# A residual convolution block with merged VectorE passes, an accumulating transfer for the input's sum, and five column-filtered positions

## The chip, the cores and the metric

The kernel runs on one core of a Trainium2 chip. The metric is the device time of one execution in microseconds (us). Before the change three runs took 1788.07, 1795.76 and 1796.89 us, with a median of 1795.76 us.

## The reference

The program is a network of four residual layers on an input of 4 images x 256 channels x 56 x 56, all in 32-bit floats. Each layer is `x = x + layer(groupnorm(x))`:

- Layers 0 and 2 are involutions: a per-pixel 7 x 7 kernel is computed from the pixel and applied to its neighbourhood.
- Layer 1, which the change is about, is a pair of 3 x 3 convolutions with batch norms:

```python
h = relu(bn(conv3x3(x, w1), g1, b1, rm1, rv1))
h = bn(conv3x3(h, w2), g2, b2, rm2, rv2)
return relu(x + h)          # x here is the group-normed input
```

  so the layer's result is `x + relu(gn(x) + bn(conv(relu(bn(conv(gn(x)))))))`.
- Layer 3 scales the input by two gates that come from means and a Fourier transform.

## The kernel before, in words

The three stages run one after the other: the involution of layer 0 (up to about 511 us), the convolutions of layer 1 (`conv_layer`, about 511 to 1241 us) and the involution of layer 2 with layer 3 folded in. Only `conv_layer` is touched by the change.

**Tiling.** 128 channels lie on the partitions, so an image has two blocks of input channels (`ci`) and two of output channels (`co`). An image is worked on in three chunks of rows, so there are 12 steps of each convolution. The first convolution takes 20, 18 and 18 rows (`C1_ROWS`), the second 16, 20 and 20 (`C2_ROWS`). The order is conv1(0), then conv1(i) and conv2(i-1) in turn, and conv2(11) at the end.

**Row filter.** Along a row, four outputs at a time are computed by a Winograd filter F(4,3): the row is split into four phases (columns 0, 1, 2, 3 modulo 4), and six linear combinations of them, the positions k = 0 to 5, are formed by VectorE (`transform`, lines 1322 to 1350; `input1` and `input2` call it for the two convolutions). For each position TensorE sums over 3 rows and 2 channel blocks: 6 matmuls for each `co`, 12 for a position (L1440 in conv1, L1522 in conv2). The six sums are then combined into the four output phases by VectorE. The positions are worked off in the order `KS = (1, 2, 3, 4, 0, 5)`. In the profile a 32-bit matmul appears as two.

**Column filter.** For three positions (`K2 = (1, 2, 3)`) conv1 is in addition filtered along columns, two output rows at a time (F(2,3)): VectorE makes four combinations of neighbouring rows (`columns`, L1374, in two halves), and TensorE needs 4 products x 4 matmuls = 16, each over half as many rows (L1411). The weights for it are made once by `column_weights` (lines 1257 to 1264). The first step, conv1(0), is not filtered, because the column weights are made during it. To evacuate a filtered position, ScalarE copies the first product (L1423) and VectorE combines it with the other three (L1426, L1427, L1429, L1430).

**What sets the order.** The program's order is written out by hand. Each step has a list `after` of 12 slots, and `after[n]` is run between the matmul groups: the transform of the step to come, the phases of the next chunk (`phases`, ScalarE, L1319, which reads the loaded rows in steps of four), the group norm's small steps (`norm_steps`, called through the list `slow` in slots 5 and 11), statistics of the finished rows (`stats`, L1565), loads and stores. `in_order` then pins the program order on every engine, so each engine works off its queue in the order of the code; an instruction that waits holds up all behind it.

**PSUM.** There are 8 banks, one to a tile (`one_bank`). A filtered position takes four. A norm step takes one from its matmul until VectorE reads it, one step's slot later.

**The end of conv2.** For each `co` ScalarE computes the residual `res = gn(x)` (L1507, `res` has one buffer), VectorE adds the four output phases to it in steps of four floats (`residual`, L1515, four passes), and one VectorE pass (L1558) computes `x + max(res, 0)`, which POOL's queue stores to HBM (L1559). `x` was loaded by `load_residual` (L1301) on SP's queue. The statistics of the result are taken in the same step for `co` = 0 and in the next conv2 for `co` = 1.

Of the kernel before, what the change touches and what calls it, by code (L numbers as in the profile page):

```python
# [16 lines left out]
P = 128  # L17
# [54 lines left out]
def net_kernel(  # L72
# [1109 lines left out]
    def conv_layer(xin, xout, st, ahead):  # L1182
        with ExitStack() as es:
            wpool = es.enter_context(tc.tile_pool(name="cw", bufs=1))
            work = es.enter_context(tc.tile_pool(name="cwork", bufs=2))
            mm_ps = es.enter_context(tc.tile_pool(name="cmm_ps", bufs=8, space=PSUM))

            def one_bank():
                return mm_ps.tile([P, 512], F32, name="mm")
# [5 lines left out]
            KS, K2 = (1, 2, 3, 4, 0, 5), (1, 2, 3)  # L1195
            u1_sb = wpool.tile([P, NB, 3, WPOS, C], F32, name="u1_sb")
            ux_sb = wpool.tile([P, NB, len(K2), C], F32, name="ux_sb")
            u2_sb = wpool.tile([P, NB, 3, WPOS, C], F32, name="u2_sb")


# [9 lines left out]
            last_y = wpool.tile([P, NY], F32, name="last_y")  # L1210

            def y_tile(k):
                if k < 5:
                    return room["h"][:, k * NY : (k + 1) * NY]
                return room["xr"][:, 2 * NX : 2 * NX + NY] if k == 5 else last_y
# [40 lines left out]

            def column_weights(ci, k0, k1):

                w0, w1, w2 = (u1_sb[:, ci, y, k0:k1, :] for y in range(3))
                x = ux_sb[:, ci, k0 - 1 : k1 - 1, :]  # L1260
# [5 lines left out]

            ph1 = wpool.tile([P, 4, CV_ROWS + 2, NB, WT + 1], F32, name="ph1")
            nc.gpsimd.memset(ph1[:, 0, :, :, 0:1], 0.0)
            nc.gpsimd.memset(ph1[:, 1, :, :, WT : WT + 1], 0.0)
            ph2 = wpool.tile([P, 4, H + 2, NB, WT + 1], F32, name="ph2")  # L1270
            nc.gpsimd.memset(ph2[:, 0, :, :, 0:1], 0.0)
            nc.gpsimd.memset(ph2[:, 1, :, :, WT : WT + 1], 0.0)
# [30 lines left out]
            def phases(i):  # L1303
# [8 lines left out]
                for ci in range(NB):  # L1312
                    at = ci * (CV_ROWS + 2) * W
                    xr = room["rows"][:, at : at + (hi - lo) * W].rearrange("p (r t j) -> p j r t", t=WT, j=4)
                    for j in range(4):
                        q, t0 = (j + 1) % 4, (j + 1) // 4
                        dst = ph1[:, q, r0 : r0 + hi - lo, ci, t0 : t0 + WT]
# [4 lines left out]
            def transform(v, ph, n):  # L1322

                by = [ph[:, j].rearrange("p r c t -> p (r c) t") for j in range(4)]
                d = [t[:, :, :WT] for t in by] + [t[:, :, 1:] for t in by[:2]]
                vs = [v[:, k, : n * NB] for k in range(WPOS)]
                stt(vs[4], d[2], -4.0, d[4], ALU.mult, ALU.add)
                yield
                stt(vs[3], d[1], -4.0, d[3], ALU.mult, ALU.add)
                yield  # L1330
                tt(vs[1], vs[4], vs[3], ALU.add)
                yield
                tt(vs[2], vs[4], vs[3], ALU.subtract)
                yield
                tt(vs[3], d[4], d[2], ALU.subtract)
                yield
                tt(vs[4], d[3], d[1], ALU.subtract)
                yield
                tt(vs[0], d[0], d[2], ALU.subtract)
                yield  # L1340
                stt(vs[0], vs[3], 0.25, vs[0], ALU.mult, ALU.add)
                yield
                tt(vs[5], d[5], d[3], ALU.subtract)
                yield
                stt(vs[5], vs[4], -4.0, vs[5], ALU.mult, ALU.add)
                yield
                stt(vs[3], vs[4], 2.0, vs[3], ALU.mult, ALU.add)
                yield
                stt(vs[4], vs[4], -4.0, vs[3], ALU.mult, ALU.add)
                yield  # L1350
# [5 lines left out]
            def input1(i):  # L1356
                y0, y1, _, _ = rows1(i)
                n = y1 - y0 + 2
                yield from transform(new_v((1, i)), ph1[:, :, :n], n)

            def input2(i):
                y0, y1 = C2_ROWS[i % 3]
                yield from transform(new_v((2, i)), ph2[:, :, y0 : y1 + 2], y1 - y0 + 2)

            def columns(i, k, half):
# [3 lines left out]
                v = v_of[1, i][:, k].rearrange("p (r e c) t -> p e r (c t)", e=2, c=NB)  # L1369
                d = [v[:, 0, :m], v[:, 1, :m], v[:, 0, 1 : m + 1], v[:, 1, 1 : m + 1]]  # L1370
                t = v2_of[i, k, half] = new_v2().rearrange("p (e r n) -> p e r n", e=2, n=NB * WT)
                pairs = ((1, 2, ALU.add), (2, 1, ALU.subtract)), ((0, 2, ALU.subtract), (1, 3, ALU.subtract))
                for e, (p, q, op) in enumerate(pairs[half]):
# [384 lines left out]
```

## Time and profile before

| | |
|---|---|
| median of three runs | 1795.76 us (1788.07 to 1796.89) |
| profiled execution | 1790.97 us |
| its span, first to last instruction | 1788.9 us |
| mean granted TensorE clock | 0.983 |
| TensorE matmul busy | 1719.6 us (96%) |
| VectorE busy | 1385.5 us (77%) |
| ScalarE busy | 814.5 us (46%) |
| GpSimd (POOL) busy | 377.3 us (21%) |
| stretch of the convolutions | about 511 to 1241 us |

PE is TensorE's matmul row, PEld its weight loads, DVE VectorE, ACT ScalarE, POOL GpSimd and SP the queue that issues most transfers. In a line of a group, the numbers after the count are the busy time in us and the mean length of one in ns, then the idle time before it and who ended it. In a timeline the first number is the start and the second the length, in us. Instructions on one engine overlap a little: the distance from start to start is what one costs in a full queue.

### The profile page before, as it was taken

Reading aid. Unit: us, or ns where it says so; the run is one execution under the profiler, and the core shown is the slowest. Engines: PE = TensorE matmul, PEld = TensorE weight load, DVE = VectorE, ACT = ScalarE, POOL = GpSimd, SP = SyncE. Lnnn points to the kernel's source line nnn. Section 1 sums busy time; section 2 is a strip of 40 time slices with the busy share of each in tenths; the row PEclk is TensorE's granted clock in tenths of the full one; section 3 lists DMA queues with packets and bytes.
Section 4 is the critical chain, followed back from the end, with each engine's and each line's share of the span. In section 5 each row is a group of like instructions: output and inputs, shape, how many; then the busy total and the mean of one; then the engine's idle time right before and its main releaser. Section 6 shows DMA issues by size and latency. Waiting matters only on the chain.

```text
span 1788.9 us, 55629 instructions
## 1 busy us (share of the span) xinstructions
PE 1719.6 (96%) x24040; PEld 1510.4 (84%) x24040; DVE 1385.5 (77%) x2745; ACT 814.5 (46%) x1882; POOL 377.3 (21%) x571
## 2 busy tenths in 40 slices
PE   6999999999999999999999999999999999899898
PEld 4988988989978988898889888986888887788786
DVE  2677787767778988988898889885787787677675
ACT  2655556555533223231323132112767567567564
POOL 2223321333210000000000000001000464553572
PEclk9999999999989999999999999999999999999996
DMA  2345444634653121211111111122345566665653
GB/s 86 127 159 166 137 151 136 197 107 131 208 158 104 39 67 57 71 43 54 64 64 46 50 64 37 45 111 72 126 161 166 166 215 206 194 202 186 181 157 114
DMA packets 67907, 215.74 MB, mean 121 GB/s; under 512 B 12790, under 2 KB 20479, under 8 KB 63951
## 3 DMA queue, kind: packets, MB, share of 16 engines
q1 hardware_dynamic: 54750, 159.83, 28.4%
q0 software_dynamic: 11072, 50.32, 8.2%
q8 instruction: 189, 3.10, 0.7%
q10 hardware_dynamic: 1840, 2.05, 0.4%
q14 instruction: 56, 0.45, 0.1%
HBM read 76.30 MB, written 49.15 MB: 70 GB/s over the span
## 4 chain that ended last, share of the span: by engine, by line
PE 68%; DVE 18%; DMA 4%; issue 4%; ACT 3%; POOL 1%; SPq 1%; ACTq 0%; DVEq 0%; POOLq 0%
PE mm L1522 17%; PE ps L592 14%; PE ps L634 13%; PE mm L1440 10%; DVE kt L610 5%; PE mm L1411 5%; DMA xw<-xw 4%; PE ps L406 3%; DVE un L654 3%; PE ps L468 2%; DVE res L1515 1%; DVE xs L1374 1%; DVE st L1104 1%; ACT hp L487 1%; PE ps L717 1%
## 5 line engine op out<-in xcount | busy, mean ns | idle before, releaser
L634 PE MATMUL ps<-kt,xw 126*32 126x48 f32 (+1 forms) x12544 | 379.9, 235 | 25.9 <-issue 13.4
L634 PEld LDWEIGHTS ps<-kt,xw 126*32 126x32 f32 (+1 forms) x12544 | 341.2, 121 | 71.5 <-issue 49.9
L592 PE MATMUL ps<-hp,z_sb 64*126 64x133 f32 x6144 | 384.1, 279 | 8.8 <-DVE kt L610 5.1
L592 PEld LDWEIGHTS ps<-hp,z_sb 64*126 64x126 f32 x6144 | 364.5, 186 | 24.7 <-DVE kt L610 6.9
L1522 PE MATMUL mm<-v,u_sb 128*128 128x280 f32 (+1 forms) x1728 | 383.5, 383 | 1.9 <-DVE u_sb L1253 1.5
L610 DVE TENSOR_TENSOR kt<-ps,zb_sb 126x798 f32<-126x798 f32 x352 | 333.0, 980 | 60.4 <-PE ps L592 60.1
L1522 PEld LDWEIGHTS mm<-v,u_sb 128*128 128x128 f32 x1728 | 326.1, 189 | 56.3 <-DVE u_sb L1253 1.9
L603 ACT ACTIVATE kt<-ps,zb_sb 126x133 f32<-126x133 f32 x960 | 280.8, 442 | 107.6 <-PE ps L592 107.6
L1440 PE MATMUL mm<-v,u_sb 128*128 128x252 f32 (+1 forms) x936 | 209.5, 384 | 0.0
L1440 PEld LDWEIGHTS mm<-v,u_sb 128*128 128x128 f32 x936 | 176.4, 189 | 30.5 <-issue 0.8
L654 DVE SCALAR_TENSOR_TENSOR un<-ps,s,un 128x240 f32<-128x240 f32 x224 | 102.5, 458 | 85.2 <-ACT un L649 78.8
L654 DVE SCALAR_TENSOR_TENSOR un<-ps,par_sb,un 128x240 f32<-128x240 f32 x224 | 97.7, 456 | 83.7 <-ACT un L647 79.8
L1559 POOL DMA_DIRECT2D x<-xs x24 | 13.2, 548 | 681.3 <-DVE xs L1558 426.5
L1507 ACT ACTIVATE res<-xs,shift,norm_sb 128x1120 f32<-128x1120 f32 (+1 forms) x24 | 30.2, 1258 | 236.9 <-DVE xs L1558 107.3
L418 ACT COPY xw<-ps 126x896 f32<-126x896 f32 x112 | 101.4, 906 | 40.7 <-PE ps L406 21.3
L659 POOL TENSOR_TENSOR xs<-un,xs 128x240 f32<-128x240 f32 x112 | 72.2, 666 | 218.6 <-DVE un L654 218.6
L406 PE MATMUL ps<-ident_sb,strip_sb 128*126 128x128 f32 x784 | 111.0, 282 | 5.3 <-issue 1.7
L647 ACT ACTIVATE un<-ps,par_sb 128x240 f32<-128x240 f32 x112 | 50.3, 449 | 120.5 <-PE ps L634 106.9
L649 ACT ACTIVATE un<-ps,bn_t,s 128x240 f32<-128x240 f32 x112 | 60.0, 538 | 92.8 <-PE ps L634 82.0
L1411 PE MATMUL mm<-xs,u_sb 128*128 128x126 f32 (+1 forms) x792 | 98.7, 277 | 2.0 <-DVE xs L1427 1.0
L406 PEld LDWEIGHTS ps<-ident_sb,strip_sb 128*126 128x126 f32 x784 | 84.3, 141 | 16.5 <-POOL strip_sb L391 4.2
L1411 PEld LDWEIGHTS mm<-xs,u_sb 128*128 128x128 f32 x792 | 94.4, 191 | 3.3 <-DVE xs L1427 1.6
(255 smaller groups left out, 1882.2 us busy)
## 6 DMA issues: line engine op xcount, KB each, us to landing
xw<-xw SPq DMA_DIRECT2D x224, 252.0 KB
xw<-xw SPq DMA_DIRECT2D x224, 126.0 KB
xs<-x SPq DMA_DIRECT2D x24, 560.0 KB
x<-xs POOLq DMA_DIRECT2D x8, 1568.0 KB, 7.8
xs<-x SPq DMA_DIRECT2D x8, 1568.0 KB
xs<-in_x_dram SPq DMA_DIRECT2D x6, 1568.0 KB
x<-xs SPq DMA_DIRECT2D x6, 1568.0 KB
gx<-x POOLq DMA_DIRECT2D x42, 224.0 KB, 5.2
```

What stands on the lines that cost most here:

```text
L406: nc.tensor.transpose(ps[:Q, k * P : (k + 1) * P], flat[:, k * Q : (k + 1) * Q], ident_sb)
L418: nc.scalar.copy(xw[:, :NSB, :], ps[:Q, : NSB * P].rearrange("q (n c) -> q n c", n=NSB))
L592: nc.tensor.matmul(ps[:Q, i, k * NT : (k + 1) * NT], z_sb[i * R : (i + 1) * R, cb * GB // 2 + gp, z0 : z0 + Q], hp[i * R : (i + 1) * R, py ...
L603: nc.scalar.activation(kt[:, g0 + i, pb, :, k], ps[:Q, i, k * NT : (k + 1) * NT], AF.Identity, bias=zb_sb[:, cb * GB + g0 + i, p0 + k : p0 ...
L610: nc.vector.tensor_tensor(kt[:, g0 : g0 + 2, pb], ps[:Q, :, : PB * NT].rearrange("q i (k t) -> q i t k", k=PB), zb_sb[:, cb * GB + g0 : cb ...
L634: nc.tensor.matmul(v[m * j : m * j + m, i, :, k * TP : (k + 1) * TP], xw[:, window(ty), m * j : m * j + m], kt[:, ng * j : ng * j + ng, :, ...
L649: nc.scalar.activation(part, o[0], AF.Identity, bias=bn["t4"][:, cb : cb + 1], scale=bn["s4"][ng][:, 0, cb : cb + 1])
L654: nc.vector.scalar_tensor_tensor(part, o[e], s, part, ALU.mult, ALU.add)
L659: nc.gpsimd.tensor_tensor(dst, u, dst, ALU.add)
L1411: nc.tensor.matmul(ps[:, co * m : (co + 1) * m], u[ci][:, co * P : (co + 1) * P], v2[:, e, : n // 2, ci * WT : (ci + 1) * WT], start=(ci = ...
L1440: nc.tensor.matmul(ps, u1_sb[:, ci, dy, k, co * P : (co + 1) * P], v[:, k, dy * NB + ci : (dy + n - 1) * NB + ci + 1 : NB, :], start=(j == 0),
L1522: nc.tensor.matmul(ps, u2_sb[:, ci, dy, k, co * P : (co + 1) * P], v[:, k, dy * NB + ci : (dy + n - 1) * NB + ci + 1 : NB, :], start=(j == 0),
```

## The change

All of it is in `conv_layer`.

- **PSUM** becomes four tiles of two banks (`two_banks`); `one_bank` hands out the first half of such a pair, so the norm steps take a pair each. An unfiltered position puts both `co` in one pair and is evacuated by VectorE passes over both. A filtered position takes two pairs (`inner`, `outer`); the signs and halves are folded into the weights (`filter_weights`), so that the outer products are added by one pass over both banks.
- **Five positions** of conv1 are filtered along columns: `K2 = (1, 2, 3, 4, 0)`. The last five of their ten half-columns are made inside conv1 (`LATER`). The between-weights of position 0 lie behind the loaded rows (`ux0_sb`).
- **`transform`** works in nine passes in place of twelve, three of them over two planes, by a layout of the phases (`PL`) and positions (`VP`) that gives two planes a constant distance.
- **Factors** 6 and 24 of the edge positions are multiplied into the weights by ScalarE (`edge_weights`), for both convolutions.
- **conv2** runs positions 1 to 4 for both `co`, then positions 0 and 5 for one `co` after the other. Its four output phases lie side by side, so one VectorE pass (`joined`) adds them to `res`, which ScalarE now writes phase by phase (reading in steps of four floats). ReLU moves to ScalarE, which writes it back in steps of four.
- **The sum with x** is done by a transfer on POOL's queue that adds the rows from HBM to the tile; the store follows it on the same queue.
- **Places:** the statistics of both `co` move into the next conv1 (slots 2, 3, 7, 8) or, at the end, the last conv2; the residual loads move into slots 0 and 1 (7 and 8 in the last conv2).

```diff
-            mm_ps = es.enter_context(tc.tile_pool(name="cmm_ps", bufs=8, space=PSUM))
+            mm_ps = es.enter_context(tc.tile_pool(name="cmm_ps", bufs=4, space=PSUM))
+            def two_banks():
+                return mm_ps.tile([P, 2, 512], F32, name="mm")
             def one_bank():
-                return mm_ps.tile([P, 512], F32, name="mm")
+                return two_banks()[:, 0, :]
-            KS, K2 = (1, 2, 3, 4, 0, 5), (1, 2, 3)
+            KS, K2 = (1, 2, 3, 4, 0, 5), (1, 2, 3, 4, 0)
...
+            def edge_weights(u, ci):
+                for k, by in ((0, 6.0), (5, 24.0)):
+                    nc.scalar.mul(u[:, ci, :, k, :], u[:, ci, :, k, :], by)
+            def filter_weights(ci, k0, k1):
+                ws = (u1_sb[:, ci, 1, k0:k1, :], 0.5), (between_weights(ci, k0, k1), 0.5), (u1_sb[:, ci, 2, k0:k1, :], -1.0)
+                for w, by in ws:
+                    nc.scalar.mul(w, w, by)
...
+                for k, p0, p1, e in ((3, 2, 0, 1), (4, 1, 3, 0)):
+                    d, far = (rows[:, PL[j], :, z : z + WT] for j, z in ((p0, 0), (p1, e)))
+                    stt(one(k), d, -4.0, far, ALU.mult, ALU.add)
+                    yield
+                tt(one(1), one(3), one(4), ALU.add)
+                yield
+                tt(one(2), one(3), one(4), ALU.subtract)
+                yield
+                tt(planes(0, 5), d01, d23, ALU.subtract)
+                yield
+                tt(planes(3, 4), d45, d23, ALU.subtract)
+                yield
+                stt(planes(0, 4), planes(3, 4), 0.25, planes(0, 5), ALU.mult, ALU.add)
+                yield
+                stt(one(3), one(5), -2.0, one(3), ALU.mult, ALU.add)
+                yield
+                stt(one(5), one(5), 4.0, one(3), ALU.mult, ALU.add)
...
             FIRST = [(K2[0], 0), (K2[0], 1), (K2[1], 0), (K2[1], 1), (K2[2], 0)]
+            LATER = {0: [(K2[2], 1)], 1: [(K2[3], 0), (K2[3], 1)], 2: [(K2[4], 0), (K2[4], 1)]}
...
+                        inner, outer = two_banks(), two_banks()
+                        work4 = ((inner, 0, va, 0, u1), (inner, 1, va, 1, ux), (outer, 0, vb, 0, u0), (outer, 1, vb, 1, u2))
...
+                        for late in LATER.get(n_s, ()):
+                            columns(i, *late)
                         h = new_half()[:, : NB * m]
-                        nc.scalar.copy(h, m1)
+                        nc.scalar.copy(h, inner[:, 0, : NB * m])
...
+                        tt(o[:, 0], rows_of(h), m2, ALU.add)
+                        tt(o[:, 1], rows_of(h), m2, ALU.subtract)
+                        run_all(after[2 * n_s])
+                        tt(o, o, outer[:, :, : NB * m].rearrange("p e (r t) -> p e r t", t=WT), ALU.add)
...
+                def joined(co):
+                    y = room["h"][:, : 4 * NY].rearrange("p (j n) -> p j n", j=4)[:, :, co * m : (co + 1) * m]
+                    rj = res.rearrange("p (j q) -> p j q", j=4)
+                    stt(rj, y, s2_6[:, co : co + 1], rj, ALU.mult, ALU.add)
+                    x = xr_of[i, co][:, : n * W]
+                    nc.scalar.activation(x.rearrange("p (q j) -> p j q", j=4), rj, AF.Relu)
+                    at = slice(y0 * W, y1 * W)
+                    nc.gpsimd.dma_start(x, xin[bb][co][:, at], accum_op=ALU.add)
+                    nc.gpsimd.dma_start(xout[bb][co][:, at], x)
...
+                residual(0)
                 for co in range(NB):
+                    pair = two_banks()
+                    at = slice(co * m, (co + 1) * m)
+                    unfiltered(pair[:, 0, :m], u2_sb, v, 0, co, n)
+                    stt(p[:, at], p[:, at], -0.75, pair[:, 0, :m], ALU.mult, ALU.add)
+                    stt(p[:, at], r[:, at], 0.25, p[:, at], ALU.mult, ALU.add)
+                    run_all(after[8 + 2 * co])
+                    unfiltered(pair[:, 1, :m], u2_sb, v, 5, co, n)
+                    stt(q[:, at], q[:, at], -3.0, pair[:, 1, :m], ALU.mult, ALU.add)
+                    stt(q[:, at], t[:, at], 4.0, q[:, at], ALU.mult, ALU.add)
+                    joined(co)
+                    if co == 0:
+                        residual(1)
+                    run_all(after[9 + 2 * co])
...
+            T2_AT = (2, 3, 7, 8)
...
+                    for at, f in zip(T2_AT, tail2):
+                        after[at].append(f)
-                        place(after, input2(j), (1, 1, 3, 3, 5, 5, 6, 7, 8, 9, 10, 10))
+                        place(after, input2(j), (1, 1, 2, 3, 5, 7, 8, 9, 10))
...
+                        for ci in range(NB):
+                            after[2 + ci].append(lambda ci=ci: edge_weights(u1_sb, ci))
+                            after[10 + ci].append(lambda ci=ci: filter_weights(ci, 1, 5))
+                            after[10].append(lambda ci=ci: column_weights(ci, 0, 1))
+                            after[11].append(lambda ci=ci: filter_weights(ci, 0, 1))
...
-                        place(after, input1(j), [1 + k // 2 for k in range(12)])
+                        place(after, input1(j), (0, 0, 1, 1, 2, 3, 4, 5, 6))
```

## The prediction

> **What bounds the kernel now.** I read the busy table and its forty slices first, then the busy time of single stretches, then the weight loads and VectorE's order in one convolution step.
>
> ```profile
> PE 1719.6 (96%) x24040; PEld 1510.4 (84%) x24040; DVE 1385.5 (77%) x2745; ACT 814.5 (46%) x1882; POOL 377.3 (21%) x571
> PE   6999999999999999999999999999999999899898
> DVE  2677787767778988988898889885787787677675
> ```
>
> TensorE is busy throughout, and in the convolutions (slices 12 to 27, 524 to 1241 us) VectorE is nearly as busy: two engines near their limit. By stretches (first conv1 of 20 rows, its conv2, then conv1 of 18 rows, its conv2 of 16):
>
> ```profile
> core 0: us, PE busy (x) PEld busy (x) DVE busy (x) ACT busy (x) POOL busy (x), PEclk, DMA share, GB/s
> 676.40:704.80 28.40, 28.40 (x169) 25.05 (x168) 25.29 (x46) 8.87 (x12) 0.54 (x1) 1.00 0.23 80
> 704.80:738.80 34.00, 34.00 (x146) 27.24 (x145) 28.09 (x59) 6.91 (x13) 0.53 (x1) 1.00 0.10 34
> 738.80:764.80 26.00, 26.00 (x169) 24.31 (x168) 22.47 (x46) 8.40 (x12) 0.53 (x1) 1.00 0.26 87
> 764.80:792.10 27.30, 27.30 (x146) 27.23 (x145) 23.53 (x51) 6.25 (x13) 0.55 (x1) 1.00 0.10 35
> ```
>
> TensorE never rests and its clock is 1.00, so time saved there counts, but only while VectorE empties PSUM soon enough. The price of a position comes from the starts of the weight loads (the timeline of an 18-row conv1; a matmul of the code is two in the profile):
>
> ```profile
> 739.79 0.97 PEld L1411 LDWEIGHTS mm<-xs,ux_sb 128*128 128x128 f32 x8
> 743.37 0.97 PEld L1411 LDWEIGHTS mm<-xs,ux_sb 128*128 128x128 f32 x8
> 749.62 15.18 PEld L1440 LDWEIGHTS mm<-v,u_sb 128*128 128x128 f32 x72
> 764.82 1.35 PEld L1522 LDWEIGHTS mm<-v,u_sb 128*128 128x128 f32 x7
> ```
>
> A filtered position takes 743.37 - 739.79 = 3.58 us, an unfiltered one (764.82 - 749.62)/3 = 5.07. The same lines of the 20-row step at 676.40 give 3.81 and 5.62. VectorE's order as another 18-row conv1 begins (TensorE entered it at 1093.05):
>
> ```profile
> 1096.85 1.33 DVE L1558 SCALAR_TENSOR_TENSOR xs<-res,xs 128x1120 f32<-128x1120 f32 x1
> 1098.09 0.74 DVE L1374 TENSOR_TENSOR xs<-v 128x252 f32<-128x252 f32 x2
> 1098.76 0.41 DVE L1426 TENSOR_TENSOR hp<-xs,mm 128x252 f32<-128x252 f32 x1
> 1099.20 0.42 DVE L1427 TENSOR_TENSOR xs<-xs,mm 128x252 f32<-128x252 f32 x1
> 1099.54 0.41 DVE L1429 SCALAR_TENSOR_TENSOR hp<-hp,mm 128x252 f32<-128x252 f32 x1
> 1099.86 0.41 DVE L1430 SCALAR_TENSOR_TENSOR hp<-xs,mm 128x252 f32<-128x252 f32 x1
> 1100.19 0.68 DVE L1327 SCALAR_TENSOR_TENSOR v<-ph 128x504 f32<-128x504 f32 x1
> 1100.79 0.68 DVE L1329 SCALAR_TENSOR_TENSOR v<-ph 128x504 f32<-128x504 f32 x1
> ```
>
> Two things: VectorE first touches conv1's PSUM 5.7 us after TensorE began, still busy with conv2's end; and starts lie 0.33 us apart at 252 elements (0.44 where one needs its predecessor), 0.60 at 504, likewise 0.71 at 616 and 0.31 for statistics of 224. Twice the length saves some 0.06 us.
>
> **The change, part by part.**
>
> 1. *Positions 4 and 0 of conv1 filtered* (11 of 12 steps; the first stays unfiltered). TensorE saves 2 x (8 x 1.49 + 3 x 1.81) = 34.7 us. This is the gain on offer.
>
> 2. *VectorE's work.* conv2 gets lighter: four stride-4 additions of 0.73 and one of 1.33 per half become one contiguous pass of 1.33, the rest are merged; some 28 us fall to 22. But conv1 gets heavier. An 18-row step after: five half-columns 3.1, five evacuations of 1.43 (252, 252, 504) 7.2, combinations 7.0 (ten of 504), the transform as six single and three double passes 8.3, statistics, now all placed in conv1, 3.1: 28.7 us, against 5 x 3.58 + 5.07 = 23.0 us of TensorE. Before, the stretch held 22.5 against 26.0. VectorE becomes the slower engine inside conv1; conv2 pays the lag back (22 in 34), which hides nothing in conv1.
>
> 3. *A new wait at the seam of conv2 and conv1.* ReLU moves from VectorE to ScalarE, and ScalarE's order at the seam is: ReLU of half 0, residual of half 1 (one buffer `res`), ReLU of half 1, then the copy of conv1's first bank. VectorE's joining pass of half 1 waits for the residual, and its first evacuation for the copy; behind that evacuation its whole queue stands. Both ScalarE passes step by four floats on one side. Bounds for 1120 elements:
>
> ```profile
> L1319 ACT ACTIVATE ph<-xs,norm_sb 128x280 f32<-128x280 f32 x32 | 26.5, 894 | 4.1 <-DVE v L1343 4.1
> L1479 ACT ACTIVATE ph<-hp,bn_t,s 128x280 f32<-128x280 f32 x8 | 4.6, 623 | 0.0
> L1507 ACT ACTIVATE res<-xs,shift,norm_sb 128x1120 f32<-128x1120 f32 x16 | 21.1, 1321 | 157.4 <-DVE xs L1558 69.9 <-DVE gm L220 42.8 <-DMA xs<-x 32.3
> L281 ACT COPY xs<-mm 126x384 f32<-126x384 f32 x1 | 1.1, 1100 | 2.0 <-PE mm L273 2.0
> ```
>
> Contiguous: 1.32. Reading in steps of four (L1319; 266 and 294 elements take 873 and 919, so 1.64 ns each): 2.27. Writing in long steps (L281, 2.6 to 2.9 ns each): 3.1. I take 2.3 for both, L1319 being the only row with this step. From TensorE's end of conv2 (0): joining pass of half 0 ends at -3.05 (its bank comes 5.7 earlier, two passes of 280, one of 1120), ReLU -0.7, residual 1.65, joining pass 3.05, ReLU 5.4, copy 5.8: first evacuation at 5.85. With ReLU at 1.32 it is 4.4, at 3.1 7.3. After a 16-row conv2: 5.1.
>
> The Trainium skill ("SBUF — State Buffer", the note on 16-byte cachelines under "Door 1") says that each access which crosses into a new 16-byte line pays a penalty, and makes no difference between reads and writes. L1319 against L1479 (894 to 623 ns) agrees for a read; no run here shows the write. By the rule both passes pay, and the sum is mine or the high end; by rows alone the write may be free, the low end.
>
> 4. *How far TensorE may run ahead.* PSUM becomes four pairs of banks; a filtered position takes two. So the fifth position (k = 0) starts only when VectorE has evacuated the third. From the first evacuation to there lie, in order: the first's three passes 1.4, two of the transform 1.4, columns 1.3, evacuation 0.8, statistics 0.6, transform 0.7, addition and combinations 2.1, statistics 0.8, transform 0.7, columns 1.3, evacuation 0.8: 11.7 us (20 rows 12.7). TensorE arrives at 4 x 3.58 = 14.3 (15.3). Wait: 5.85 + 11.6 - 14.3 = 3.1 in steps 4, 7, 10; 2.5 in 5, 8, 11 (after 16 rows); 3.3 in step 3; 3.6 in step 2 (lag from the start-up). A step saves 3.0 or 3.6: nearly nothing is left. From there position 5 and conv2 find their banks free.
>
> 5. *Norm steps.* Two PSUM tiles are held from the end of conv2 into the third position of steps 6 and 9. Of four pairs two are left, and every position waits for the last: by the same walk 7.0 us of wait each (before, with 8 banks, 0.5). Each norm also delays the conv2 before it by some 1 us, three times.
>
> 6. *Start-up.* After step 0 VectorE must make filters for two more positions (six passes 256 longer, six new: 4.2 us) and ScalarE scale them (twelve passes, 9 us; the last 1024-wide one ends 4.6 us after TensorE is done; before, 1.0 idle). conv1 step 1 then carries 12 passes of 768 for the second weights (0.96 each) on a VectorE already full. Walking the queue, TensorE ends the first conv2 at 622.9 instead of 615.5: 10.4 us of wait against the 3.0 saved.
>
> 7. *Accumulating transfer.* VectorE's sum x becomes a POOL transfer that adds from HBM, and the store waits for it on the POOL queue, with the powers of the norms behind. Plain POOL writes of 560 KB land in 3.0 us, the slowest POOL rows in 7.8. Statistics ask for it 11.4 us after ReLU: no cost up to there; each us beyond costs one in ten steps. I take 0. The residual loads move on SP from conv2's entry to its first two slots, 22 us ahead of their reader (in the last conv2 behind the statistics, still some 5 us ahead), and the scaling of the edge weights is eight ScalarE passes of 768 while ScalarE is idle two thirds of the time: 0 as well; uncovered they would cost some 3 us and 7 us, once.
>
> 8. *End.* The last ReLU stands before layer 2's first ScalarE work, and five more statistics in its first images: 1.5.
>
> Sum: -34.7 + waits (3.6 + 3.3 + 9.3 + 7.5 + 14.0 = 37.7, less 1.9 already there) 35.8 + 10.4 + 3 + 1.5 = +16. The profiled execution took 1790.97 us (span 1788.9, 2.1 around it): 1807. The median of the three runs shown is 4.8 higher, so I put the median at 1809.
>
> **Rivals.** *Cheap ScalarE* (0.17): writing in steps costs nothing; the first evacuation at 4.4 takes 1.45 off ten steps: +1.5, 1792 to 1797. For: only reading is shown slow; against: L281. *VectorE keeps up* (0.11, faster): if the passes overlap better than their spacing shows, so that first evacuation plus walk is below 14.3 us, TensorE keeps the 34.7 less 8 of start-up: 1764 to 1770. It decides from a first evacuation at 2.6 us; against it, before already has 5.7. *Late accumulation* (0.14): landing at 16 us gives (16 - 11.4) x 10 = 46 more, 1855. For: it reads its destination too; against: 7.8 is the slowest plain one.
>
> **How the numbers follow.** My case has 0.58; with ReLU from 1.6 to 3.1 us it spans 1797 to 1828. The range 1787 to 1842 takes in the cheap case and the first part of a late accumulation, leaving out the faster case. About 0.5% (9 us) is what a measurement can tell. Faster 0.14: the keep-up case and the edge of the cheap one. Same 0.26: most of the cheap case and the lower edge of mine. Slower 0.60.
>
> **What would show it.** Filtered positions at 3.6 and 3.8 us; TensorE waiting in conv1 before its fifth position on VectorE, some 3 us, 7 in steps 6 and 9; VectorE above 95% in conv1 and idle in conv2; ScalarE passes of 2.3 us; VectorE waiting for ScalarE at conv1's first evacuation. I am wrong if conv1 runs near 23 us without waits, or if VectorE waits for a transfer at the statistics.

## The result, and the profile after

The changed kernel takes 1842.66 us (median of 4 runs, 1836.18 to 1845.58), the kernel before in the same comparison 1791.91 us: a ratio of 1.0285, 95% interval 1.0229 to 1.0342. It is 51 us slower where 13 were forecast, and 0.7 us above the top of the stated range. The profiled execution has a span of 1840.8 us against 1788.9.

The page of the changed kernel first, its busy table and the slices of TensorE and VectorE:

```profile
PE 1712.9 (93%) x24216; PEld 1507.1 (82%) x24216; DVE 1357.4 (74%) x2527; ACT 908.5 (49%) x1922; POOL 400.6 (22%) x595
PE   6999999999998899999899889999899989999998
DVE  2777777776689878787877786774677777777685
```

Between slice 12 and slice 28 (the convolutions) TensorE now has slices of 8, and VectorE isn't busier than before but idler (74% against 77%): neither engine is busy throughout any more. They wait for each other. The convolutions end at 1291.9 us instead of 1242.2, and layer 2 takes 548.9 us after them against 546.7; nearly all of the loss is in the convolutions.

The same kind of stretches as in the prediction (conv1 of 20 rows, its conv2, conv1 of 18 rows, its conv2 of 16), cut where TensorE goes from one to the next:

```profile
core 0: us, PE busy (x) PEld busy (x) DVE busy (x) ACT busy (x) POOL busy (x), PEclk, DMA share, GB/s
687.30:716.20 28.90, 26.68 (x186) 25.38 (x185) 25.98 (x47) 13.70 (x19) 1.97 (x3) 0.94 0.55 138
716.20:752.29 36.09, 34.45 (x146) 27.02 (x145) 24.62 (x39) 9.30 (x9) 0.86 (x1) 1.00 0.05 16
752.29:777.65 25.36, 23.25 (x186) 22.51 (x185) 22.42 (x46) 13.15 (x19) 2.00 (x3) 1.00 0.62 158
777.65:807.02 29.37, 27.76 (x145) 27.02 (x144) 23.95 (x40) 7.95 (x9) 0.66 (x1) 1.00 0.06 16
```

conv1 gains next to nothing, as forecast: 28.90 us against 28.40 before in the 20-row step, 25.36 against 26.00 in the 18-row step. What wasn't forecast stands in the other two rows: each conv2 is 2.1 us longer than before (36.09 against 34.00, 29.37 against 27.30), though VectorE is less busy in the first of them (24.62 against 28.09). And in the first row the granted clock is 0.94.

The longer conv2 and the lower clock are both seen in the timeline of TensorE's matmuls from the end of one conv2 to the end of the next conv1 (in brackets the idle time ahead of a row and what ended it; L1420 is an unfiltered position, L1458 a filtered one; `...` stands for rows left out):

```profile
1123.28 5.93 PE L1420 MATMUL mm<-v,u_sb 128*128 128x280 f32 x24 [1.09 <-DVE hp L1573]
1129.74 3.10 PE L1420 MATMUL mm<-v,u_sb 128*128 128x280 f32 x12 [0.54 <-DVE hp L1573]
1132.68 1.05 PE L1458 MATMUL mm<-xs,u_sb 128*128 128x126 f32 x8
...
1145.18 1.95 PE L1458 MATMUL mm<-xs,u_sb 128*128 128x126 f32 x16
1149.26 1.74 PE L1458 MATMUL mm<-xs,u_sb 128*128 128x126 f32 x8 [2.13 <-DVE hp L1473]
1150.79 1.92 PE L1458 MATMUL mm<-xs 128*128 128x126 f32 x8
```

Three things. The fifth position waits 2.13 us for the evacuation of the third (line 1473), as forecast at 3.1. Ahead of k = 5 of each half of conv2, TensorE waits 1.09 and 0.54 us for line 1573, which reads k = 0 of that half: a wait that the prediction doesn't have. And the eight matmuls behind the long wait take 1.74 and 1.92 us where the same eight take 1.05 at 1132.68. The granted clock in two such places, after a wait of 2.11 us at 958.2 and after another of 2.11 us at 769.0:

```profile
957.20:958.20 1.00, 0.00 (x0) 0.02 (x1) 0.90 (x4) 0.00 (x0) 0.00 (x0) 1.00 0.00 0
958.20:961.60 3.40, 3.39 (x17) 3.40 (x18) 3.26 (x6) 0.00 (x0) 0.00 (x0) 0.54 0.00 0
...
769.00:772.40 3.40, 3.32 (x30) 3.35 (x31) 3.22 (x6) 1.14 (x2) 0.00 (x0) 1.00 0.00 0
```

After the first, 17 matmuls go through in 3.4 us at a clock of 0.54; after the second, 30 at 1.00. In the convolutions of this profile 11 of the 12 waits of 2.08 us or more are followed by some 3.4 us at half clock, and none of the 16 waits between 1.09 and 1.69 us. Each such stretch costs 3.4/2 = 1.7 us, 11 of them 18.7.

With this the convolutions can be balanced, 718.1 us before (524.1 to 1242.2) against 769.0 after (522.9 to 1291.9). TensorE's idle time goes from 4.4 to 63.5 us: ahead of the fifth position 14.7 in eight steps and 10.2 in steps 6 and 9; at the three entries of a conv2 with norms 7.8; ahead of k = 5 in conv2 23.0, of them 5.1 in the first one; at the start of step 1 and ahead of its fifth position 7.2. Its busy time falls by 8.1 instead of 34.7, and 18.7 of the missing 26.6 are the half clock. The remaining 8 aren't taken apart by any run. Some of it may be matmuls starting anew after a wait, since a conv2 is 2.1 us longer while its two waits sum to 1.6; that is not shown.

### The profile page after: what moved, and what is told of

The parts are those of the page before. It is cut to its first block, busy times and chain, and to the rows that moved or that the text cites. A ratio compares the mean times of both kernels' runs of the same rounds, so it can differ in the third digit from the quotient of the medians.

```text
span 1840.8 us, 55893 instructions
## 1 busy us (share of the span) xinstructions
PE 1712.9 (93%) x24216; PEld 1507.1 (82%) x24216; DVE 1357.4 (74%) x2527; ACT 908.5 (49%) x1922; POOL 400.6 (22%) x595
## 3 DMA queue, kind: packets, MB, share of 16 engines
q0 software_dynamic: 14528, 63.16, 12.5%
## 4 chain that ended last, share of the span: by engine, by line
PE 59%; DVE 24%; ACT 5%; issue 5%; DMA 4%; SPq 2%; POOL 1%; ACTq 0%; DVEq 0%; POOLq 0%
PE mm L1420 22%; PE ps L592 14%; PE ps L634 12%; DVE kt L610 5%; DMA xw<-xw 4%; PE mm L1458 3%; PE ps L406 3%; DVE un L654 2%; PE ps L468 1%; ACT xs L1536 1%; DVE xs L1399 1%; SPq L424 1%; DVE v L1362 1%; DVE res L1534 1%; SPq L425 1%
## 5 line engine op out<-in xcount | busy, mean ns | idle before, releaser
L1420 PE MATMUL mm<-v,u_sb 128*128 128x280 f32 (+2 forms) x2136 | 489.3, 389 | 29.3 <-DVE hp L1573 23.0
L1420 PEld LDWEIGHTS mm<-v,u_sb 128*128 128x128 f32 x2136 | 405.7, 191 | 108.6 <-DVE hp L1573 32.9
L1458 PE MATMUL mm<-xs,u_sb 128*128 128x126 f32 (+1 forms) x1320 | 171.3, 284 | 32.1 <-DVE hp L1473 27.3
L1458 PEld LDWEIGHTS mm<-xs,u_sb 128*128 128x128 f32 x1320 | 163.3, 198 | 35.0 <-issue 30.0
L1538 POOL DMA_DIRECT2D xs<-x x24 | 21.6, 901 | 506.0 <-ACT xs L1536 505.9
L1536 ACT ACTIVATE xs<-res 128x1120 f32<-128x1120 f32 (+1 forms) x24 | 50.2, 2091 | 162.0 <-DVE res L1534 162.0
L149 POOL TENSOR_TENSOR norm_sb<-norm_sb,mhalf 128x1 f32<-128x1 f32 x32 | 20.6, 646 | 440.3 <-DVE norm_sb L148 440.3
L1437 ACT ACTIVATE ph<-hp,bn_t,s 128x252 f32<-128x252 f32 (+1 forms) x96 | 52.0, 606 | 85.7 <-DVE hp L1498 56.6
```

The source lines that it names most:

```text
L1420: nc.tensor.matmul(ps, *position(u, v, ci, dy, k, co, n), start=(j == 0), stop=(j == NB * 3 - 1))
L1458: nc.tensor.matmul(ps[:, bank, co * m : (co + 1) * m], u[ci][:, co * P : (co + 1) * P], v2[:, e, : n // 2, ci * WT : (ci + 1) * WT], start ...
L1536: nc.scalar.activation(x.rearrange("p (q j) -> p j q", j=4), rj, AF.Relu)
```

## The experiments

The theory after reading the trace: three separate waits (a PSUM pair shared by two positions; the ScalarE chain at the seam; pairs held by the norms), each made dearer by the half clock, and a start-up, rather than one engine that has too much work. Times are medians, ratios stand against the kernel before, with 95% intervals. The changed kernel has 1.0285. The kernel before was run anew beside each group of experiments, with medians from 1787.20 to 1791.91 us; by the ratios the gains of 1 to 5 over the changed kernel come out 1 to 3 us smaller than by the medians. Code that is left out of a diff is marked by `...`.

**1. A PSUM pair of its own for k = 5.**

```diff
-                    unfiltered(pair[:, 1, :m], u2_sb, v, 5, co, n)
-                    stt(q[:, at], q[:, at], -3.0, pair[:, 1, :m], ALU.mult, ALU.add)
+                    last = two_banks()
+                    unfiltered(last[:, 0, :m], u2_sb, v, 5, co, n)
+                    stt(q[:, at], q[:, at], -3.0, last[:, 0, :m], ALU.mult, ALU.add)
```

> One edit to the changed kernel: in the second convolution the sixth position (k = 5) gets a PSUM pair of its own instead of the second bank of the pair that holds position 0. Theory (shared pair): the 0.5 to 1.2 us that TensorE waits for VectorE (line 1573) ahead of each k = 5 exists only because the matmul into one bank waits for the reader of the other bank of the same pair. Then all 24 of these waits vanish, and each second convolution loses the 2.1 us that it is longer than before (5 us in the first one): 28 us. Part comes back: the ScalarE chain at the seam doesn't get shorter by it, so TensorE ends the second convolution some 0.7 us further ahead of it and waits 0.7 us longer ahead of the fifth position of each of ten first convolutions, and where that makes the wait longer than about 2.1 us the granted clock falls to 0.5 for 3.4 us, 1.7 us more in up to five further steps. Expected 1826 to 1832, 1.019 to 1.023 of the kernel before. Rival (VectorE is truly late): the waits move to the next position or stay, 1838 to 1845. Rival (nothing comes back): 1812 to 1816.

Measured: 1821.14 us, 1.0179 (1.0159 to 1.0199), 21.5 less and 5 below the expected range. TensorE's timeline of this kernel in the same place:

```profile
1094.67 14.78 PE L1420 MATMUL mm<-v,u_sb 128*128 128x280 f32 x62
1109.29 1.05 PE L1458 MATMUL mm<-xs,u_sb 128*128 128x126 f32 x8
...
1126.36 2.01 PE L1458 MATMUL mm<-xs,u_sb 128*128 128x126 f32 x8 [2.62 <-DVE hp L1473]
```

The waits inside conv2 are gone, all 24. So VectorE wasn't late: a matmul into bank 1 waited because VectorE was still reading bank 0 of the same tile. The wait ahead of the fifth position grew, as expected, but only from 2.13 to 2.62 us here. From the first filtered matmul to the end of the convolutions the kernel is 28.4 us shorter (700.9 against 729.3), with the longer waits ahead of the fifth position already taken off. What came back lies elsewhere: layer 2 is 12.5 us longer in this profile (561.4 against 548.9). Its opening has a wait of 5.23 us for a strip from GpSimd (POOL): the strip stands behind the second store on GpSimd's queue here (1275.68, then 1276.32), in the changed kernel ahead of it (1301.60, then 1304.94). Experiment 9 takes this up; the rest of the 12.5 I can't place. After the end of the convolutions the profiles of the changed kernel and the eleven experiments spread over 545 to 562 us, with no cause found for some 5 us either way.

**2. ReLU of half 1 behind ScalarE's first copy.** Its two transfers go with it; `finish` holds all three. The last two conv2 stay as they were.

```diff
                         nc.scalar.copy(h, inner[:, 0, : NB * m])
+                        run_all(held)
...
-                    nc.scalar.activation(x.rearrange("p (q j) -> p j q", j=4), rj, AF.Relu)
...
+                    if co and i < n_chunks - 2:
+                        held.append(finish)
+                    else:
+                        finish()
```

> One edit to the changed kernel: at the seam, ReLU of half 1 and its two transfers are issued after ScalarE's copy of the first bank of the next first convolution instead of ahead of it. Theory (ScalarE chain at the seam): VectorE's first evacuation, 5.36 us after TensorE began in the trace, comes 1.85 us earlier, and all VectorE work up to the third evacuation with it; the waits ahead of the fifth position fall from 1.5 to 2.2 us to 0 to 0.4, and the 3.4 us at half the granted clock that follow the waits over 2.1 us go too (five steps, 1.6 us each). 17 + 8 = 25 us less: 1815 to 1821. Rival (VectorE's amount of work bounds the first convolution, wherever it begins): at most 5 us less, 1837 to 1843.

Measured: 1822.95 us, 1.0180 (1.0156 to 1.0204), 19.7 less. ScalarE's order at the seam in the changed kernel (residual of half 1, ReLU of half 1, copy of conv1's first bank), then VectorE's, first of the changed kernel and then of this one:

```profile
1131.13 2.41 ACT L1522 ACTIVATE res<-xs,shift,norm_sb 128x1120 f32<-128x1120 f32 x1
1135.34 2.24 ACT L1536 ACTIVATE xs<-res 128x1120 f32<-128x1120 f32 x1 [1.80 <-DVE res L1534]
1137.39 0.41 ACT L1468 COPY xs<-mm 128x252 f32<-128x252 f32 x1
```

```profile
1133.92 1.39 DVE L1534 SCALAR_TENSOR_TENSOR res<-hp,s,res 128x1120 f32<-128x1120 f32 x1
1135.23 0.68 DVE L1399 TENSOR_TENSOR xs<-v 128x504 f32<-128x504 f32 x1
1137.83 0.42 DVE L1472 TENSOR_TENSOR hp<-xs,mm 128x252 f32<-128x252 f32 x1 [1.93 <-ACT xs L1468]
```

```profile
1119.36 1.39 DVE L1537 SCALAR_TENSOR_TENSOR res<-hp,s,res 128x1120 f32<-128x1120 f32 x1
1120.66 0.68 DVE L1399 TENSOR_TENSOR xs<-v 128x504 f32<-128x504 f32 x1
1121.26 0.41 DVE L1473 TENSOR_TENSOR hp<-xs,mm 128x252 f32<-128x252 f32 x1
```

VectorE's 1.93 us of waiting for the copy are gone, and so are the waits ahead of the fifth position in steps 2 to 5, 7, 8, 10 and 11: not one above 0.25 us is left. So the seam's chain set them, not the amount of VectorE's work. The gain is 2 us below the lower end of what was expected; steps 6 and 9 kept 0.6 and 3.1 us of their 5.1.

**3. The norms inside one conv2.**

```diff
                 for g in slow:
-                    after[5].append(step(g))
-                    after[11].append(step(g))
+                    for at in (5, 11) if i < 3 else (1, 3, 5, 7, 9, 11) if conv == 2 else ():
+                        after[at].append(step(g))
...
```

> One edit to the changed kernel: the six steps of the norms of the last layer's inputs are spread over one second convolution (slots 1, 3, 5, 7, 9, 11) instead of two steps a convolution over three, so that no PSUM pair is held across a seam. Theory (held pairs): three second convolutions lose the 0.53 + 2.08 us that TensorE waits at their entry and the 1.6 us at half the clock that follow; steps 6 and 9 lose 3 us of their waits each (5.1 us, down to the 2.1 of the other steps). 13 + 6 = 19 us less: 1821 to 1826. Rival (the tiny matmuls of the norms wait for VectorE wherever they stand): the waits stay in another place, 1836 to 1845.

Measured: 1828.63 us, 1.0214 (1.0191 to 1.0238), 14.0 less; between the ranges of the theory and its rival, 3 above the theory's. The entry of the conv2 that carries norms, in the changed kernel:

```profile
832.76 0.35 PE L217 MATMUL mm<-mv,gavg_sb 128*128 128x1 f32 x2 [0.53 <-DVE xs L1473]
835.20 5.02 PE L1420 MATMUL mm<-v,u_sb 128*128 128x280 f32 x13 [2.08 <-DVE xs L1475]
```

Both waits are gone in the experiment, with the half clock behind them, in all three places: 13 us. In steps 6 and 9 the two earlier waits fell from 2.0 to 0.9 us together, but the one ahead of the fifth position stayed at 3.12. There the edit put a new wait in place of the one that it removed: at the seam VectorE now waits for a power of the norm on GpSimd.

```profile
876.50 0.16 DVE L232 SCALAR_TENSOR_TENSOR norm_sb<-gm,norm_sb 128x1 f32<-128x1 f32 x1 [3.56 <-POOL norm_sb L149]
877.01 0.16 DVE L232 SCALAR_TENSOR_TENSOR norm_sb<-gm,norm_sb 128x1 f32<-128x1 f32 x1 [0.35 <-POOL norm_sb L149]
```

So the held pairs explain the entries; for steps 6 and 9 this run can't tell, since the later start of VectorE alone would give them a wait. Experiment 2 has the other half: there the pairs are still held, VectorE waits for nothing on GpSimd in step 6, and TensorE waits 3.12 us there as well. Experiment 9 has neither.

**4. Positions 4 and 0 unfiltered, all else as changed.**

```diff
-            KS, K2 = (1, 2, 3, 4, 0, 5), (1, 2, 3, 4, 0)
+            KS, K2 = (1, 2, 3, 4, 0, 5), (1, 2, 3)
...
```

The half-columns and filter weights of the two positions go with them.

> The changed kernel with positions 4 and 0 of the first convolution unfiltered, as before; pairs, longer passes, ScalarE's work and the adding transfer stay. TensorE's work grows by 34.7 us (1.49 or 1.81 us for two positions in eleven steps). Theory (the fifth position's saving is eaten by its waits): the waits ahead of the fifth position go (15 us in eight steps, some 6 us in steps 6 and 9), with them the stretches at half clock (5 us), and the preparation of the further filters (some 8 us of waiting in step 1): 34.7 - 34 = about +1, 1838 to 1850. Rival (filtering two more positions is what made the kernel slower): 1800 to 1815. Rival (their 34.7 us were kept in full): 1872 to 1880.

Measured: 1819.03 us, 1.0167 (1.0148 to 1.0186), 23.6 less: a miss. I expected the two positions to pay for themselves; as changed they cost 24 us. The trace shows two terms that I had too small. TensorE leaves the first conv2 at 614.9 us instead of 626.4, though step 1 has 3.0 us more of matmuls: the filters for two more positions cost some 14 us of start-up, not 8. (Its wait ahead of k = 5, 4.65 us against 1.13 here, is part of them.) And all half-clock stretches are gone, in steps 2 to 11 and at the entries. So the first rival, that filtering two more positions made the kernel slower, is the nearest, 4 us above its range, and explains 24 of the 51 us. It doesn't say why; experiments 7 and 10 do.

**5. The edits of 1, 2 and 3 together.**

> The three edits together (own PSUM pair for k = 5 in the second convolution; ReLU of half 1 issued after ScalarE's first copy; norms within one second convolution). Theory (three separate waits, and halves of the clock that follow them): the gains of the single edits, 20, 18 and 12 us, add up, and the part of the first that came back as longer waits ahead of the fifth position (some 8 us with the half clock) is saved as well: 50 to 60 us below the changed kernel, 1781 to 1793, 0.995 to 1.002 of the kernel before. What is left above a full saving lies in the start-up, some 11 us. Rival (one resource, VectorE's work in the first convolution, stands behind all three): the edits overlap, 1805 to 1818.

Measured: 1795.37 us, 1.0039 (1.0022 to 1.0055), 47 less than the changed kernel, 2 above the range. The single gains were 21.5, 19.7 and 14.0, in sum 55: they add up but for 8 us (by the ratios 50 and 44), so the rival with one resource behind all three (1805 at the least) is out.

**6. Later preparation of the filters.** As 5; step 1 leaves positions 4 and 0 unfiltered, and their filters are made in the first conv2.

```diff
-                    if k in K2 and i > 0:
+                    if k in (K2[:3] if i == 1 else K2) and i > 0:
...
+                            for at, k in ((ci, 4), (2 + ci, 0)):
+                                after[at].append(lambda ci=ci, k=k: column_weights(ci, k, k + 1))
+                                after[at + 2].append(lambda ci=ci, k=k: filter_weights(ci, k, k + 1))
```

> As the kernel with the three edits, and the preparation of the filters of positions 4 and 0 moves from the end of step 0 into the first second convolution; step 1 leaves these two positions unfiltered. Theory (start-up is bounded by VectorE's and ScalarE's preparation): the kernel with three filtered positions ended the first second convolution 11 us earlier, with 3.0 us more TensorE work in step 1; some 3 to 5 us of it come back because VectorE prepares the filters in that second convolution, where it is busy 34 of 40 us. 6 to 9 us below the kernel with the three edits, 1773 to 1786. Rival (the preparation only moves the wait): within 2 us of it.

Measured: 1787.40 us, 0.9998 (0.9975 to 1.0020): 8.0 less than 5, the gain as expected and the sum 1 above its range. TensorE's waits at the start of step 1 (6.5 us in 5) and ahead of its fifth position are down to 0.9.

**7. As 5, with three filtered positions.** The edit of 4 on top of 5.

> As the kernel with the three edits, but positions 4 and 0 unfiltered in all steps. Theory: with the waits gone TensorE's work decides again. Ten steps lose 3.15 us each, less some 1 us each that may still wait ahead of the fifth position, and the start-up gains 11 us: 10 to 20 us above the kernel with the three edits, 1795 to 1808. Rival (filtering the two positions costs as much as it saves, whatever the waits): within 5 us of the kernel with the three edits, or faster.

Measured: 1791.39 us, 1.0025 (1.0008 to 1.0042), 4 us below 5, where 10 to 20 above were expected: a miss again, and the rival's side. The three-position kernel carries no start-up, so 6 is the fair comparison, and five positions are 4 us better there by the medians, 10 by the two profiled executions. Of the 31.7 us that ten steps have on offer, waits still eat a large part: those of 0.2 us or more in the convolutions sum to 18.9 us in 6 and to 5.7 here. The trace of 6 shows which, at the seam of step 6 (first GpSimd's, then VectorE's rows):

```profile
851.83 0.55 POOL L1544 DMA_DIRECT2D x<-xs  x1 [5.69 <-DMA xs<-x]
852.39 1.10 POOL L149 TENSOR_TENSOR norm_sb<-norm_sb,mhalf 128x1 f32<-128x1 f32 x2
```

```profile
853.01 0.16 DVE L232 SCALAR_TENSOR_TENSOR norm_sb<-gm,norm_sb 128x1 f32<-128x1 f32 x1 [4.18 <-POOL norm_sb L149]
853.52 0.16 DVE L232 SCALAR_TENSOR_TENSOR norm_sb<-gm,norm_sb 128x1 f32<-128x1 f32 x1 [0.35 <-POOL norm_sb L149]
```

The store (line 1544 here) stands 5.69 us at the head of GpSimd's queue until the adding transfer has landed. The powers of the norms (line 149) stand behind it, VectorE waits 4.18 us for them, and its first evacuation of conv1 stands behind that. At the opening of layer 2 TensorE waits 6.09 us for a strip that stands behind the other store.

**8. No adding transfer** (the sum with x is left out).

```diff
-                    nc.gpsimd.dma_start(x, xin[bb][co][:, at], accum_op=ALU.add)
```

> The changed kernel without the adding transfers: the sum with x is left out, ReLU's result is stored and measured by the statistics as it is. Theory (the transfer is hidden, as predicted: it lands 5.2 to 7.2 us after its issue, and no statistics wait for it): within 4 us of the changed kernel, 1837 to 1846. Rival (it delays something on its queue or shares DMA bandwidth that the loads of the rows need): 10 us or more below the changed kernel.

Measured: 1843.82 us, 1.0310 (1.0283 to 1.0338). In the changed kernel the transfer costs nothing that can be measured, as predicted. That is so because nothing in its convolutions waits for what stands behind the transfer on GpSimd's queue, and no property of the transfer: with edit 3 VectorE waits 3.56 us for a power that now stands behind it, and with edit 1 TensorE waits 5.23 us for a strip that stands behind the store.

**9. GpSimd's queue kept free.** As 6; powers ahead of the adding transfers, and x added by VectorE in the last conv2.

```diff
-                    for at in (5, 11) if i < 3 else (1, 3, 5, 7, 9, 11) if conv == 2 else ():
+                    for at in (5, 11) if i < 3 else (0, 2, 3, 5, 7, 9) if conv == 2 else ():
...
+                    if i == n_chunks - 1:
+                        xj = x.rearrange("p (q j) -> p j q", j=4)
+                        stt(xj, rj, 0.0, xj, ALU.max, ALU.add)
+                        nc.gpsimd.dma_start(xout[bb][co][:, at], x)
+                        return
```

> As the kernel with the three edits and the later preparation of the filters (1787), with two edits against waits on POOL's queue: the norms' powers are issued before the adding transfers of their second convolution (slots 0, 2, 3, 5, 7, 9), and the last second convolution adds x by VectorE, as before, instead of by a transfer. Theory (POOL's queue: the store stands there until the adding transfer has landed, and the powers and the strips of layer 2 stand behind it): VectorE loses the 4.2 us that it waited for a power ahead of its first evacuation in steps 6 and 9, TensorE there 1.3, 0.3 and 3.1 us of waits down to 0.7, and the half clock behind one of them; the opening of layer 2 loses 4.5 us of TensorE's 6.1 us wait for a strip and the half clock behind it. 10 + 6 us less, 1768 to 1776, 0.989 to 0.994 of the kernel before. Rival (other work takes the place of the powers and strips): within 4 us of 1787.

Measured: 1766.50 us (6 runs), 0.9895 (0.9871 to 0.9919), 21 less than 6, 1.5 below the expected range, and 1% faster than the kernel before. GpSimd's rows around the same seam:

```profile
836.99 1.58 POOL L149 TENSOR_TENSOR norm_sb<-norm_sb,mhalf 128x1 f32<-128x1 f32 x2 [37.92 <-DVE norm_sb L148]
844.61 0.90 POOL L1549 DMA_DIRECT2D xs<-x  x1 [6.04 <-ACT xs L1548]
850.86 0.55 POOL L1550 DMA_DIRECT2D x<-xs  x1 [5.34 <-DMA xs<-x]
```

The powers are done 6 us before the transfer is issued. Steps 6 and 9 now wait 0.72 us ahead of their fifth position, like the others (0.42 to 0.72, only step 2 has 2.68); conv1 of the three 20-row steps 3, 6 and 9, cut where TensorE enters and leaves it, reads:

```profile
675.66:701.54 25.88, 25.16 (x186) 23.84 (x185) 24.37 (x45) 14.47 (x19) 2.61 (x4) 1.00 0.59 154
844.84:870.72 25.88, 25.16 (x186) 23.85 (x185) 24.37 (x45) 14.48 (x19) 2.68 (x4) 1.00 0.59 154
1014.00:1039.90 25.90, 25.18 (x186) 23.85 (x185) 24.36 (x45) 14.50 (x19) 2.71 (x4) 1.00 0.61 154
```

Such a step took 28.40 us before and 28.90 in the changed kernel; here it takes 25.9. The clock is 1.00, TensorE is busy 25.2 us of it and VectorE 24.4: now both are near their limit, and most of the two positions' saving (2.5 of 3.6 us) is kept.

**10 and 11. As 9, with three and with four filtered positions** (10 by the edit of 4; 11 leaves position 0 unfiltered).

> As the last, but with positions 4 and 0 unfiltered in all steps. Theory: only without the waits do the two positions pay. Against the kernel with the three edits and three positions (1791) it gains the 6 us at the opening of layer 2 and 1.5 us each in steps 6 and 9: 1780 to 1785, some 10 us above five positions. Rival (the two positions bring nothing): as five positions within 3 us.

> As the first of these three, but with position 0 unfiltered in all steps. Theory: TensorE has 16 us more (1.49 or 1.81 us in ten steps) and loses 0.4 to 0.7 us of waiting ahead of the fifth position in each: 8 to 12 us above five positions. Rival (VectorE's smaller work is worth it): at most equal to five positions.

Measured: 1782.71 us, 0.9982 (0.9966 to 0.9999), and 1778.86 us, 0.9957 (0.9934 to 0.9980), each of 12 runs: 16 and 12 us above five positions, 10 inside its range and 11 just above its own (8 to 12). The same two positions cost 24 us in the kernel as changed (4) and bring 16 here. For 10 the profiles place 19.7 us in the convolutions; for 11 they place only 4.4 (665.23 against 660.87 from the first filtered matmul on); the rest lies in layer 2, whose code is the same, so the 12 us are the kernel's time but not shown to be position 0's alone.

## Why the prediction was right and wrong

- *Step 1, the saving on offer*: right. Filtered positions take 3.57 and 3.81 us, and 10 against 9 shows that they pay once TensorE needn't wait.
- *Step 2, VectorE the slower engine inside conv1*: wrong. I summed 28.7 us for an 18-row conv1 and 22 for a 20-row conv2; the stretches show 22.4 and 24.6. As they are cut at TensorE and VectorE lags, only their sums compare well, 47.0 against 50.7. VectorE is busy 88 and 90% of conv1 where above 95% was to show it, and 597.3 us of the convolutions where it was 621.8 before. Experiment 2 removed the waits without removing work, so VectorE's amount of work wasn't what bound conv1.
- *Step 3, the seam*: right. First evacuation 5.4 us after TensorE's entry (1137.83 less 1132.44) against 5.85 (the 1132.44 is where its weight loads enter); the ScalarE passes take 2.42 us (reading in steps of four) and 2.23 (writing) against 2.3 each. This settles what the trace of before left open: the write in steps is as dear as the read, which is the side of the Trainium skill's note ("SBUF — State Buffer", "Door 1") that no row then showed. The cheap-ScalarE rival falls with it.
- *Step 4, the wait ahead of the fifth position*: mechanism right (experiment 2), 14.7 us in eight steps where the terms summed to 23.7. The walk of 11.7 us took 11.4 (its terms as printed sum to 11.9, and the waits were worked out with 11.6), and the first evacuation came half a microsecond earlier. Its last sentence, "From there position 5 and conv2 find their banks free", is **the step that failed**: I followed the pairs by when they come free from one position to the next, and not inside a pair. k = 0 and k = 5 of a half share one, and the matmul waits for the reader of the other bank. This term was put at nothing; the waits sum to 23.0 us, and experiment 1 makes the convolutions 28 us shorter by removing them.
- *Step 5, pairs held by norms*: mechanism right, 10.2 us against 14 in steps 6 and 9, but 7.8 against 3 at the entries. Experiment 3 removes the entries' part; with pairs held but nothing awaited from GpSimd (experiment 2) step 6 waits 3.12 us ahead of its fifth position, and with both free (experiment 9) steps 6 and 9 wait 0.72 us like the others.
- *Step 6, start-up*: the end of the first conv2, put at 622.9 us, came at 626.4. The 10.4 us of wait that I counted are some 14 by experiment 4. They contain the wait ahead of k = 5 in this conv2 (4.65 us), which I hadn't counted, and three stretches at half clock.
- *Step 7, the adding transfer at nothing*: right for this kernel (experiment 8; it lands 5.2 to 7.2 us after its issue, well before the 11.4 that the prediction allowed). The prediction names the powers behind it on GpSimd's queue; nothing waits for them in this kernel, and experiments 3, 7 and 9 show what it costs once an edit puts them right behind the transfer.
- *Step 8, the end*: 2.2 us against 1.5.
- *What no step has*: the clock. Every price in the sum was taken at a granted clock of 1.00, because the trace of before shows nothing else in the convolutions. That was the state of an engine that hardly waited (4.4 us in all, none above 1.50); the change made it wait. 11 stretches at half clock are 18.7 us.

The sum was +16; 23 us for the shared pair and 19 for the clock were missing from it, which makes 58 against the 52 by which the profiled span grew; the other terms were too large by some 14 us, and the 8 us that stay unplaced make up for part of that. That the measured time lies within 1 us of the range's top is luck: the range went that far for a late accumulation, and none came. That rival's 1855 is the nearest of the rivals' times, by none of its reasoning.

## What to carry to other kernels

When buffers are merged (two PSUM banks into one tile), list for every tile who writes one part while another part is read: a wait by tile is paid there, even when each part by itself is free. Price each new wait of TensorE of about 2 us or more, or two shorter ones close together, with the half clock that may follow, so 2 us can count as nearly 4, and look for the shortest edit that brings it under that. A transfer that costs nothing is priced anew when an edit puts other work behind it on its queue: what counts is who waits for what stands there.

## What the runs showed of the hardware

- *The clock falls after short waits.* Over the convolutions of the twelve profiles (the changed kernel and the experiments), 40 of the 57 waits of TensorE between 1.75 and 3.2 us are followed by half clock, and all 10 longer ones. Of those between 1.0 and 1.75 us only two are (at the start of step 1), and both stand next to a second wait of 0.9 us. Waits of the same 2.11 us fall on both sides. The Trainium skill ("TensorE: Matmul & The Clock Gate", "Part 1: The HAM clock gate") gives a free-running window of some 3.4 us. The traces agree: in each profile all changes of the clock lie on one grid of 3.413 us, to within 2 ns. In the grid's windows around the two waits of 2.11 us, the first wait lies within one window and the second doesn't:

```profile
955.04:958.45 3.41, 1.30 (x12) 1.14 (x11) 3.31 (x9) 1.27 (x2) 0.00 (x0) 1.00 0.43 172
958.45:961.87 3.42, 3.42 (x18) 3.42 (x18) 3.28 (x6) 0.04 (x1) 0.00 (x0) 0.50 0.00 0
...
767.30:770.71 3.41, 1.63 (x14) 1.66 (x15) 3.31 (x7) 0.00 (x0) 0.00 (x0) 1.00 0.03 9
770.71:774.13 3.42, 3.42 (x27) 3.28 (x26) 3.25 (x7) 1.14 (x2) 0.00 (x0) 1.00 0.26 42
```

TensorE idles 2.11 us in the first window and 1.78 in the second. Of some 2500 windows at full clock in the convolutions of the twelve profiles, all 49 with 2.02 us or more of idle time are followed by half clock, none of those with 1.79 or less is, and of the 6 between 3 are. So what counts is the idle time within a window, about 1.9 us of 3.41, and not the length of one wait. The skill's rule against idle gaps above 3.4 us (same page, "HAM oscillation") is too lenient by these traces: a wait of 2.08 us was enough.

- *ScalarE writing in steps of four floats* takes 2.23 us for 1120 elements, reading so 2.42; its contiguous pass of that size in the trace of before took 1.32.
- *An adding transfer* of 560 or 448 KB from HBM into SBUF lands in 5.2 to 7.2 us (median 5.8); the plain store of 560 KB in 3.1.
